# A two-layer Mamba/attention kernel on one core: where the two layer norms of layer 1 get their sums, and new due times

## The chip, the cores and the metric

One Trainium2 chip, one of its cores. A core has TensorE (PE in the profile), VectorE (DVE), ScalarE (ACT), GpSimd (POOL) and a queue engine, SyncE (SP), that here issues almost all DMAs. Each engine works through its own instructions in program order and waits on semaphores for the others. The metric is the device time of one execution in microseconds (us), less is better; all data is fp32.

## The reference

The input `x` has 8 images of 384 channels and 32 x 32 = 1024 positions. Layer 0 is an RMS norm, a Mamba block run forwards and backwards over the 1024 positions (16 states a channel), and a gated depthwise 3 x 3 convolution, all added to `x`. Layer 1 works on tokens and is

```python
t = _to_tokens(x)
t = t + _L1_attn_ref(_ln_t(t), L1_attn_Wq, L1_attn_Wk, L1_attn_Wv)
t = t + _L1_ffn_ref(_ln_t(t), L1_ffn_c_fc_1, L1_ffn_c_fc_2, L1_ffn_c_proj_1, L1_ffn_c_proj_2)

def _ln_t(v, eps=1e-5):
    m = jnp.mean(v, axis=-1, keepdims=True)
    s = jnp.var(v, axis=-1, keepdims=True)
    return (v - m) / jnp.sqrt(s + eps)
```

The attention is causal with 64-wide rotated queries and keys; the feed-forward has 1536 hidden units, an exact GELU, and weights that are Kronecker products. The change touches only how `m` and `s` of `_ln_t` are made (two norms, each over 384 channels of 8 x 1024 tokens, so 128 tiles of 128 tokens in all) and when things are scheduled.

## The kernel before, in words

**Staging.** The eight images are a software pipeline. For image `b` the scan of layer 0 runs in four steps (`STEPS`: two halves of 512 positions, backwards and forwards), each of 12 units (`NU * SG`, three channel tiles times four state groups), so 48 units an image and 384 in all. One unit (`scan`) is: a GpSimd product `hs = du * br` over 128 x 2048; four ScalarE exponentials `da = exp(dl * nega)` into PSUM; four VectorE scans (`tensor_tensor_scan`); the product with `cr`, on VectorE in four pieces or, for the units in `POOL_C`, on GpSimd in one piece; and four TensorE matmuls with `sel` that add the states up into the PSUM bank `y`. While one image scans, the next image's norm, projections and convolutions (`arrive`, `conv_tokens`, `prepare`, `local_branch`) and the previous image's layer 1 (`attention`, `feed_forward`) are laid between its units. After the last image's scan only its own layer 1 is left.

**What sets the order.** No engine's order is written out. Every call goes through `plan.scalar`, `plan.vector` and so on, and is recorded with a due time in scan units (`plan.due`) and a priority bonus (`plan.rush`). `Plan.order()` then schedules all recorded operations with its own costs, one list per engine, and `issue()` emits them in that order; that is why nearly every row of the profile has line L494, the one call in `issue()`. An operation's rank is its due less its rush: among those that could start, the lowest rank goes first. The constants at the head of the file are such due times: `FIRST`, `SECOND`, `OTHERS` for the next image's preparation, `PROJECT` for the last projection of layer 0, `LAYER1` and `LAYER1_7` for attention and feed-forward, `EXPS` the rush of the exponentials, `SCAN` the offsets within a unit, `DU_AHEAD` and `DL_AHEAD` how far ahead the scan's inputs are loaded. `PATIENCE` and `YIELD` weigh a switch of ScalarE's function table. There are five PSUM banks for `da` (`DAS`), two for everything else (`w`) and one for `y`. Where TensorE would idle long enough to lose clock, the planner puts in matmuls by zero (`y<-zero,ident`).

**The lines around the change.** `project` (L1171) writes one tile of the layer-1 input, `t1[:, ti]` (128 tokens x 384 channels), by a ScalarE copy out of PSUM. `token_norm` (from L1175) makes the statistics of `nt` tiles (4, or 2 in the last half): per tile a VectorE `bn_stats` and `bn_aggr`, which give mean and variance; then on ScalarE `Ln` and `Exp` (the power -1/2), an operation `minus`, and one 128 x 1 operation per tile for the bias. `normed` applies both in one ScalarE pass into `xt` (two buffers), which TensorE transposes. `attention` adds its result to `t1` by a VectorE `scalar_tensor_tensor` (L1318), and `feed_forward` calls `token_norm` again on that. The profile calls `t1` by `t`.

Of the kernel before, what the change touches and what calls it, by code (L numbers as in the profile page):

```python
# [26 lines left out]
AF = mybir.ActivationFunctionType  # L27
ALU = mybir.AluOpType
AX = mybir.AxisListType

P = 128
# [10 lines left out]
LATER_US = 36.0  # L42


FIRST = (2.72, 6.32, 10.68, 12.81, 18.74, 20.85)
SECOND = (22.85, 0.56)
OTHERS = (
    (3.96, 9.04, 14.9, 17.84, 20.11, 24.16, 30.75, 28, 43.27, 52.42),
    (3.99, 9.04, 15.17, 17.84, 20.3, 24.1, 30.14, 30.73, 43.27, 52.45),
    (3.99, 8.8, 14.02, 17.77, 20.08, 25.25, 30.19, 27.95, 42.89, 51),  # L50
    (3.99, 9.04, 14.9, 17.84, 19.59, 24.12, 30.52, 30.81, 42.97, 52.39),
    (3.99, 8.7, 15.25, 17.84, 20.1, 24.57, 29.82, 28, 43.27, 52.42),
    (3.99, 8.21, 14.9, 17.77, 20.1, 24.12, 30.52, 26.96, 43.27, 51.49),
    (3.82, 8.84, 15.11, 17.55, 20.38, 24.12, 29.69, 27.74, 41.51, 52.45),
)
BURST = 8.31
PROJECT = (2.31, 2.01, 2.15, 1.76, 2.22, 1.78, 2.15, 2.22, 0.91)
LAYER1 = (
    (38.52, 47.93, 60.93, 69.79, 84.06),
    (38.04, 48.09, 60.67, 69.2, 83.95),  # L60
    (38.63, 48.04, 61.04, 69.31, 84.17),
    (38.33, 47.57, 60.93, 69.59, 84.06),
    (41.08, 45.96, 60.93, 69.71, 84.06),
    (38.16, 48.76, 60.73, 69.67, 83.84),
    (44.98, 47.51, 53.66, 70.69, 74.67),
)
LAYER1_7 = (39.27, 42.31, 50.52, 59.01, 62.44, 70.84, 71.42, 76.4, 81.79)
HASTE = 25.1
FREE = ["w", "da", "w", "da"]
EXPS = -0.37  # L70
SCAN = (-1.43, -1.16, -0.47, -0.43, -0.26, 0.17, 0.01, 1.1, 0.64)
DU_AHEAD = 2.82
DL_AHEAD = 2.15
DLS = 5
DAS = 5
class _Op:
# [21 lines left out]
class Plan:  # L98
# [8 lines left out]
    SWITCH = 1.4  # L107
    LOOSE = ("w", "tmp", "wt")
    HURRY = 7.14
    PATIENCE = 1.81  # L110
    TAIL = dict(tensor=0.21, vector=0.117, scalar=0.14, gpsimd=0.1, sync=0.1)
    RAW = 0.07
    NEXT = 0.01
    SIGHT = 48.0
    YIELD = 6.02
    TURN = 0.1
    RATE = 320e3
    LEAD, FIX, LAND = 1.2, 0.1, 2.0
# [379 lines left out]
def conv_attn_kernel(  # L498
# [20 lines left out]
    nc = tc.nc  # L519
    NB, C, H, W = x.shape  # L520
    L = H * W
# [13 lines left out]
    NT = HB // P  # L535
# [4 lines left out]
    l1 = ctx.enter_context(tc.tile_pool(name="l1", bufs=1))  # L540
# [18 lines left out]
    plan = Plan(nc, tc)  # L559
# [5 lines left out]
    eps = const.tile([P, 2], F32, name="eps")  # L565
# [99 lines left out]
    pa = bank()[:, : C // CG * NS]  # L665
# [481 lines left out]
    def project(b, h, t1, lo=0, hi=HB):  # L1147

        yz = [yz_t[b, h, lo, cc] for cc in range(NC)]
        wout = heavy("wout", b)  # L1150
        lx = []
        for cc in range(NC):
            lx.append((tmp()[:, : hi - lo], reps()[:, : hi - lo]))
            plan.sync.dma_start(lx[cc][0], lx_t[b, h][cc * P : (cc + 1) * P, lo:hi])
            plan.sync.dma_start(lx[cc][1], xv[b, :, cc, h * HB + lo : h * HB + hi])
        yield
        for i in range((hi - lo) // P):
            cols = slice(i * P, (i + 1) * P)
            po = bank()
            for cc in range(NC):  # L1160
                plan.tensor.matmul(
                    po[:, :C], yz[cc][:, cols], wout[:, cc], start=cc == 0, stop=False,
                    skip_group_check=True,
                )
            for cc in range(NC):
                for k in range(2):
                    plan.tensor.matmul(
                        po[:, cc * P : (cc + 1) * P], lx[cc][k][:, cols], ident, start=False,
                        stop=cc == NC - 1 and k == 1, is_transpose=True, skip_group_check=True,
                    )  # L1170
            plan.scalar.copy(t1[:, h * NT + lo // P + i], po[:, :C])  # L1171
            yield


    def token_norm(t1, ti0, nt):  # L1175

        mv = plan.tile(l1, [P, NT, 2], "mv")[:, :nt]
        for i in range(nt):
            st = plan.tile(l1, [P, nc.vector.BN_STATS_DIM], "st", 2)
            plan.vector.bn_stats(st, t1[:, ti0 + i])  # L1180
            plan.vector.bn_aggr(mv[:, i], st)
        nrm = plan.tile(l1, [P, 2, NT], "nrm", 2)[:, :, :nt]
        plan.scalar.activation(nrm[:, 0], mv[:, :, 1], AF.Ln, bias=eps[:, 1:2])
        plan.scalar.activation(nrm[:, 0], nrm[:, 0], AF.Exp, scale=-0.5)
        minus = plan.tile(l1, [P, NT], "minus", 2)[:, :nt]
        plan.scalar.activation(minus, nrm[:, 0], AF.Identity, scale=-1.0)
        for i in range(nt):
            plan.scalar.activation(
                nrm[:, 1, i : i + 1], mv[:, i, 0:1], AF.Identity, scale=minus[:, i : i + 1]
            )  # L1190
        return nrm

# [5 lines left out]
        )  # L1198
        return xt

    kv_t = {}

    def attention(b, t1, t0, n, end=False):
        if b not in kv_t:
# [4 lines left out]
        k_all, v_all = kv_t[b]  # L1209
        half = slice(t0, t0 + n)  # L1210
        tile0, nt = t0 // P, n // P
        nrm = token_norm(t1, tile0, nt)
        yield
        if end:
            xT = plan.tile(l0, [P, NQ * HB], "hs", 5)[:, : NC * n]
# [3 lines left out]
        for i in range(nt):  # L1219
            xt = normed(t1, tile0, nrm, i)  # L1220
# [45 lines left out]
        for i in range(nt):  # L1266
            ti = tile0 + i
            spans = [(s, min(s + HB, (ti + 1) * P)) for s in range(0, (ti + 1) * P, HB)]
            ng = len(spans)
            sm = plan.tile(l1, [P, 8], "sm", 2)  # L1270
            scores = []
            for g, (s0, s1) in enumerate(spans):
                pg = bank()
                diag = g == ng - 1
                plan.tensor.matmul(
                    pg[:, : s1 - s0], q[:, i * P : (i + 1) * P], k_all[:, s0:s1],
                    start=True, stop=not diag,
                )
                if diag:
                    plan.tensor.matmul(  # L1280
                        pg[:, s1 - s0 - P : s1 - s0], ident, cmask, start=False, stop=True
                    )
                plan.vector.reduce_max(sm[:, g : g + 1], pg[:, : s1 - s0], axis=AX.X)
                scores.append(pg)
            if ng == 2:
                plan.vector.reduce_max(sm[:, 3:4], sm[:, 0:2], axis=AX.X)
            top = sm[:, 3:4] if ng == 2 else sm[:, 0:1]
            plan.vector.tensor_scalar_mul(sm[:, 2:3], top, -sscale)
            pr = []
            for g, (s0, s1) in enumerate(spans):  # L1290
                pr.append(plan.tile(l1, [P, HB], "p", 2))
                plan.scalar.activation(
                    pr[g][:, : s1 - s0], scores[g][:, : s1 - s0], AF.Exp,
                    bias=sm[:, 2:3], scale=sscale, accum_out=sm[:, 4 + g : 5 + g],
                )
            yield
            total = sm[:, 4:5]
            if ng == 2:
                total = sm[:, 7:8]
                plan.vector.reduce_sum(total, sm[:, 4:6], axis=AX.X)  # L1300
            plan.vector.reciprocal(sm[:, 6:7], total)
            pT = []
            for g, (s0, s1) in enumerate(spans):
                pg = bank()
                for s in range(s0, s1, P):
                    plan.tensor.transpose(
                        pg[:, s - s0 : s - s0 + P], pr[g][:, s - s0 : s - s0 + P], ident
                    )
                pT.append(plan.tile(l1, [P, HB], "p", 2))
                plan.scalar.copy(pT[g][:, : s1 - s0], pg[:, : s1 - s0])  # L1310
            yield
            pa = bank()
            for j in range(ti + 1):
                plan.tensor.matmul(
                    pa[:, :C], pT[j // NT][:, j % NT * P : (j % NT + 1) * P], v_all[:, j],
                    start=j == 0, stop=j == ti,
                )
            plan.vector.scalar_tensor_tensor(  # L1318
                t1[:, ti], pa[:, :C], sm[:, 6:7], t1[:, ti], ALU.mult, ALU.add
            )  # L1320
            yield

    def feed_forward(b, t1, t0, n, direct=False):
        tile0, nt = t0 // P, n // P
        nrm = token_norm(t1, tile0, nt)
        yield

        xT = plan.tile(l1, [P, NF // 2, HB], "gl")[:, :NC, :n]
        for i in range(nt):
            xt = normed(t1, tile0, nrm, i)  # L1330
# [95 lines left out]
    for b in range(NB):  # L1426
# [32 lines left out]
            local_branch(b, 1, v[8], v[9])  # L1459

        t1 = plan.tile(l1, [P, L // P, C], "t1")
        for si, (d, h) in enumerate(STEPS):

            parts = ((0, HQ), (HQ, HB)) if last and si == 3 else ((0, HB),)
            for lo, hi in parts:
                e = B + (si + hi / HB) * NU * SG
                scan(b, si, lo, hi)
                if si >= 2:
                    rota[:] = FREE if last and si == 3 and hi == HB else ["w"]
                    plan.rush = HASTE if last else 0.0  # L1470
                    plan.spread(project(b, h, t1, lo, hi), e + 0.45, e + PROJECT[b + (lo > 0)])
                    plan.rush = 0.0
# [90 lines left out]
```

## Time and profile before

| | |
|---|---|
| runs | 2993.01, 2996.16, 2999.89 us; median 2996.16 |
| the profiled execution | 2996.29 us, of it span 2994.5 us from first to last instruction; mean granted TensorE clock 0.963 |
| DMA | 674.54 MB, queue of SyncE busy 67.6% of 16 engines' span |
| the four scan instructions on VectorE, busy | 631.0 + 595.0 + 325.8 + 307.0 us |
| `hs<-hs,br` on GpSimd | 399 instructions, 1739.7 us |
| `da<-dl,nega` (the exponentials) on ScalarE | 1584 instructions, 1040.5 us |
| table loads on ScalarE | 163, 1283 ns each |
| matmuls by zero on TensorE | 1620 records, 428.1 us |

A row of a group reads: line, engine, operation, output <- inputs by name, shapes, how many; then busy us and mean ns of one; then the engine's idle time just before them and what ended it. Instructions of one engine overlap a little at their ends, so busy times of groups, added up, can exceed the engine's.

### The profile page before, as it was taken

How to read it: one execution, taken by the hardware profiler on the slowest of the kernel's cores; microseconds unless marked ns; L12 is line 12 of the kernel's file. 1: busy time of each engine (PE TensorE's matmuls, PEld its weight loads, DVE VectorE, ACT ScalarE, POOL GpSimd, SP SyncE). 2: the span in 40 equal slices, each digit the busy share in tenths (PEclk: the TensorE clock that was granted, in tenths of full speed). 3: DMA queues.
4: the chain of work that ended last, by engine and by line, in shares of the span. 5: the costliest groups of instructions: out<-in, count | busy, mean ns of one | idle time of the engine just before them, and what ended most of it. 6: DMA issues, size and time to landing. Idle time of an engine off the chain costs nothing. (4 is left out here: it accounts for less than half of the span.)

```text
span 2994.5 us, 40605 instructions
## 1 busy us (share of the span) xinstructions
PE 2748.8 (92%) x12560; PEld 1245.8 (42%) x12560; DVE 2662.6 (89%) x3443; ACT 2225.2 (74%) x4166; POOL 2505.5 (84%) x692
## 2 busy tenths in 40 slices
PE   8779789999999889999999998999999998998899
PEld 4334244443444334343444434343343434444455
DVE  5799779898999899998999989999899989999971
ACT  4666567778697887878787786877778786777674
POOL 3899788698888888899988888889789889999840
PEclk9989899999999999999999999999899999999999
DMA  6778886668767687687867686676776778543510
GB/s 205 274 266 259 299 277 226 210 239 272 231 226 250 237 268 230 224 271 233 267 201 245 215 294 208 214 259 232 261 235 216 263 248 256 181 153 124 175 55 11
DMA packets 371490, 674.54 MB, mean 225 GB/s; under 512 B 44640, under 2 KB 73640, under 8 KB 371272
## 3 DMA queue, kind: packets, MB, share of 16 engines
q1 hardware_dynamic: 371144, 671.83, 67.6%
q8 instruction: 99, 1.62, 0.2%
q14 instruction: 119, 0.97, 0.1%
q0 software_dynamic: 128, 0.11, 0.0%
HBM read 505.60 MB, written 166.18 MB: 224 GB/s over the span
## 5 line engine op out<-in xcount | busy, mean ns | idle before, releaser
L494 POOL TENSOR_TENSOR hs<-hs,br 128x2048 f32<-128x2048 f32 (+2 forms) x399 | 1739.7, 4378 | 245.7 <-PE y L494 136.3
L494 ACT ACTIVATE da<-dl,nega 128x512 f32<-128x512 f32 (+1 forms) x1584 | 1040.5, 678 | 270.6 <-DVE hs L494 237.2
L494 POOL TENSOR_TENSOR hs<-hs,cr 128x2048 f32<-128x2048 f32 (+1 forms) x137 | 599.6, 4377 | 130.3 <-DVE hs L494 75.9
L494 DVE TENSOR_TENSOR_SCAN da<-da,carry,hs 128x512 f32<-128x512 f32 (+1 forms) x532 | 631.0, 1221 | 66.3 <-POOL hs L494 48.7
L494 DVE TENSOR_TENSOR hs<-da,cr 128x512 f32<-128x512 f32 (+1 forms) x1036 | 658.5, 666 | 2.1
L494 DVE TENSOR_TENSOR_SCAN da<-da,hs 128x512 f32<-128x512 f32 x504 | 595.0, 1217 | 38.9 <-ACT da L494 28.2
L494 PE MATMUL y<-hs,sel 128*32 128x512 f32 (+1 forms) x3168 | 427.3, 606 | 41.8 <-POOL hs L494 37.5
L494 PE MATMUL y<-zero,ident 128*128 128x256 f32 x1620 | 428.1, 394 | 0.0
L494 PEld LDWEIGHTS y<-zero,ident 128*128 128x128 f32 x1620 | 291.0, 193 | 160.1 <-issue 128.8
L494 DVE TENSOR_TENSOR_SCAN hs<-da,hs 128x512 f32<-128x512 f32 x264 | 307.0, 1208 | 51.0 <-ACT da L494 49.7
L494 DVE TENSOR_TENSOR_SCAN hs<-da,carry,hs 128x512 f32<-128x512 f32 (+1 forms) x284 | 325.8, 1191 | 12.6 <-ACT da L494 11.7
L494 PE MATMUL w<-xn,wt 128*128 128x512 f32 x576 | 268.0, 607 | 3.4 <-ACT tmp L494 1.7
L492 ACT ACT_TABLE_LOAD x162 | 207.8, 1283 | 2.9
L494 PE MATMUL w<-v,p 128*128 128x384 f32 x562 | 198.4, 499 | 3.9 <-ACT p L494 2.5
L494 PEld LDWEIGHTS y<-hs,sel 128*32 128x32 f32 x3168 | 90.4, 111 | 259.1 <-issue 136.4
L494 ACT COPY carry<-da 128x1 f32<-128x1 f32 x532 | 77.5, 161 | 152.6 <-DVE hs L494 151.4
L494 PE MATMUL w<-q,fc1s 32*128 32x512 f32 (+1 forms) x396 | 161.2, 679 | 28.2 <-ACT gl L494 13.4
L494 ACT COPY gl<-w 128x384 f32<-128x384 f32 (+2 forms) x317 | 160.3, 537 | 30.5 <-PE w L494 30.0
L494 PEld LDWEIGHTS w<-xn,wt 128*128 128x128 f32 x576 | 105.9, 193 | 142.9 <-issue 107.3
L494 PE MATMUL w<-rep,cit 96*32 96x512 f32 x1152 | 151.4, 639 | 4.6 <-ACT gl L494 2.8
L494 PE MATMUL y<-tmp,ddiag 128*128 128x512 f32 (+1 forms) x198 | 115.6, 669 | 43.5 <-DVE tmp L494 19.4
L494 PEld LDWEIGHTS w<-v,p 128*128 128x128 f32 x562 | 103.5, 192 | 90.3 <-ACT p L494 19.5
(187 smaller groups left out, 3349.2 us busy)
## 6 DMA issues: line engine op xcount, KB each, us to landing
hs<-db SPq DMA_DIRECT2D x372, 256.0 KB, 4.7
dl<-dd SPq DMA_DIRECT2D x372, 256.0 KB, 4.2
rep<-up SPq DMA_DIRECT2D x180, 257.5 KB, 4.2
rep<-xq SPq DMA_DIRECT2D x192, 222.4 KB, 4.8
br<-bd SPq DMA_DIRECT2D x124, 256.0 KB, 4.5
cr<-bd SPq DMA_DIRECT2D x124, 256.0 KB, 4.8
ud<-uc SPq DMA_DIRECT2D x96, 256.0 KB, 4.4
dd<-tmp SPq DMA_DIRECT2D x96, 256.0 KB, 4.0
```

The lines of the kernel that those rows point to most:

```text
L492: self.nc.scalar.preload_act_table_set(table)
L494: op.call(*args, **{k: self._bind(v) for k, v in op.kw.items()})
```

## The change

The statistics of `_ln_t` are made by ScalarE. The ScalarE pass that writes `t1` in `project` becomes an `Identity` activation with an accumulator output, the row sum; the VectorE instruction that adds attention's result to `t1` gets an accumulator output too. `token_norm` takes the sums, has VectorE multiply them by -1/C (one small instruction for all tiles of the norm: `mean` holds minus the mean), and lets ScalarE square each tile about its mean with an accumulator output, the sum of squares `var`; `1/C` goes into the scale of the `Ln`. `bn_stats`, `bn_aggr` and `minus` go. The pass of squares writes into the `xt` buffers and uses nothing of what it writes. The due times are others.

```diff
-FIRST = (2.72, 6.32, 10.68, 12.81, 18.74, 20.85)
+FIRST = (3.34, 6.32, 11.21, 12.81, 18.69, 20.85)
...
-    (3.96, 9.04, 14.9, 17.84, 20.11, 24.16, 30.75, 28, 43.27, 52.42),
+    (4.1, 9.04, 14.9, 17.84, 20.11, 24.88, 29.66, 30.73, 43.27, 52.42),
...
-BURST = 8.31
-PROJECT = (2.31, 2.01, 2.15, 1.76, 2.22, 1.78, 2.15, 2.22, 0.91)
+BURST = 7.93
+PROJECT = (2.31, 2.01, 2.22, 0.98, 1.75, 1.6, 2.15, 2.22, 0.91)
...
-LAYER1_7 = (39.27, 42.31, 50.52, 59.01, 62.44, 70.84, 71.42, 76.4, 81.79)
+LAYER1_7 = (40.42, 42.2, 51.27, 58.72, 62.92, 71.14, 71.84, 76.4, 80.71)
...
-EXPS = -0.37
-SCAN = (-1.43, -1.16, -0.47, -0.43, -0.26, 0.17, 0.01, 1.1, 0.64)
-DU_AHEAD = 2.82
-DL_AHEAD = 2.15
+EXPS = -1.3
+SCAN = (-1.43, -1.18, -0.47, -0.43, -0.26, 0.17, 0.01, 1.1, 0.66)
+DU_AHEAD = 2.93
+DL_AHEAD = 2.71
...
-    PATIENCE = 1.81
+    PATIENCE = 1.76
...
-    YIELD = 6.02
+    YIELD = 5.89
...
-            plan.scalar.copy(t1[:, h * NT + lo // P + i], po[:, :C])
+            ti = h * NT + lo // P + i
+            plan.scalar.activation(
+                t1[:, ti], po[:, :C], AF.Identity, accum_out=sums_t[b][:, ti : ti + 1]
+            )
...
-    def token_norm(t1, ti0, nt):
-
-        mv = plan.tile(l1, [P, NT, 2], "mv")[:, :nt]
+    def token_norm(b, t1, ti0, nt):
+
+        mean = plan.tile(l1, [P, NT], "mean", 2)[:, :nt]
+        plan.vector.tensor_scalar_mul(mean, sums_t[b][:, ti0 : ti0 + nt], -1.0 / C)
+        var = plan.tile(l1, [P, NT], "var", 2)[:, :nt]
         for i in range(nt):
-            st = plan.tile(l1, [P, nc.vector.BN_STATS_DIM], "st", 2)
-            plan.vector.bn_stats(st, t1[:, ti0 + i])
-            plan.vector.bn_aggr(mv[:, i], st)
+            sq = plan.tile(l1, [P, C], "xt", 2)
+            plan.scalar.activation(
+                sq, t1[:, ti0 + i], AF.Square, bias=mean[:, i : i + 1],
+                accum_out=var[:, i : i + 1],
+            )
         nrm = plan.tile(l1, [P, 2, NT], "nrm", 2)[:, :, :nt]
-        plan.scalar.activation(nrm[:, 0], mv[:, :, 1], AF.Ln, bias=eps[:, 1:2])
+        plan.scalar.activation(nrm[:, 0], var, AF.Ln, bias=eps[:, 1:2], scale=1.0 / C)
         plan.scalar.activation(nrm[:, 0], nrm[:, 0], AF.Exp, scale=-0.5)
-        minus = plan.tile(l1, [P, NT], "minus", 2)[:, :nt]
-        plan.scalar.activation(minus, nrm[:, 0], AF.Identity, scale=-1.0)
         for i in range(nt):
             plan.scalar.activation(
-                nrm[:, 1, i : i + 1], mv[:, i, 0:1], AF.Identity, scale=minus[:, i : i + 1]
+                nrm[:, 1, i : i + 1], mean[:, i : i + 1], AF.Identity, scale=nrm[:, 0, i : i + 1]
             )
         return nrm
...
             plan.vector.scalar_tensor_tensor(
-                t1[:, ti], pa[:, :C], sm[:, 6:7], t1[:, ti], ALU.mult, ALU.add
+                t1[:, ti], pa[:, :C], sm[:, 6:7], t1[:, ti], ALU.mult, ALU.add,
+                accum_out=sums_t[b][:, ti : ti + 1],
             )
...
         t1 = plan.tile(l1, [P, L // P, C], "t1")
+        sums_t[b] = plan.tile(l1, [P, L // P], "sums", 2)
```

Left out of the diff: the other six rows of `OTHERS` (the sixth entry moves from about 24.1 to about 24.9, the eighth from 27 to 30.8 to 29.8 to 30.8, the rest by some tenths), small moves in `LAYER1`, and the parameter `b` at the two calls of `token_norm`. In the built programs VectorE goes from 3445 listed instructions to 3223 (128 `bn_stats` and 128 `bn_aggr` less, 34 `mean` more), ScalarE from 4072 to 4168 (128 squares more, 34 `minus` less, table loads 163 to 165), TensorE has 825 instead of 810 matmuls by zero, GpSimd and SyncE have as many as before; accumulator reads are not among the listed ones. The order changes on every engine.

## The prediction

> **What bounds the kernel now.** I read the busy sums first, then busy times by stretch, then VectorE's waits, then the groups that the change touches. The sums of the page:
>
> ```profile
> span 2994.5 us, 40605 instructions
> ...
> PE 2748.8 (92%) x12560; PEld 1245.8 (42%) x12560; DVE 2662.6 (89%) x3443; ACT 2225.2 (74%) x4166; POOL 2505.5 (84%) x692
> ```
>
> TensorE looks fullest, but 428.1 us of its time are matmuls by zero that the planner put into gaps; without them it is at 78%. VectorE is the fullest engine with work that counts. The busy times by stretch (us from the span's start, stretch length, then busy us per engine, granted clock, DMA share, GB/s):
>
> ```profile
> 0.00:100.00 100.00, 85.59 (x266) 38.79 (x266) 63.45 (x118) 48.89 (x86) 48.51 (x28) 0.97 0.69 227
> 100.00:450.00 350.00, 284.68 (x1239) 116.30 (x1240) 285.33 (x321) 227.04 (x377) 299.41 (x87) 0.90 0.81 274
> 450.00:2880.00 2430.00, 2271.18 (x10501) 1028.26 (x10499) 2282.37 (x2931) 1885.69 (x3566) 2152.73 (x577) 0.97 0.69 228
> 2880.00:2995.00 115.00, 107.36 (x558) 62.43 (x556) 31.49 (x76) 63.59 (x140) 4.89 (x3) 0.99 0.07 22
> ```
>
> The columns are PE, PEld, DVE, ACT, POOL. In the long middle VectorE is busy 94%, GpSimd 89%, ScalarE 78%. It idles 147.6 us there; the same view in 50 us stretches shows 30 of 49 with VectorE at 47 us or more, several at the full 50. In the last 115 us it is nearly idle: the last image's layer 1 is bound by TensorE and ScalarE in turn. What VectorE waited for in the middle (us, times, longest):
>
> ```profile
> DVE hs L494 <- ACT da L494: 44.1, 22, 6.3
> DVE da L494 <- ACT da L494: 34.5, 18, 5.7
> DVE da L494 <- POOL hs L494: 24.5, 11, 9.2
> DVE tmp L494 <- PE y L494: 23.2, 11, 8.1
> ```
>
> So VectorE sets the pace of the middle, and what stops it most (78.6 us in 40 waits) is a late exponential from ScalarE, the engine that now gets more to do. The same view for GpSimd gives 104.7 us on `y` (a `hs` buffer freed by TensorE), 58.3 on VectorE and 46.2 on ScalarE's `carry`: it waits for the loop that VectorE paces.
>
> **What is taken off VectorE.** The groups:
>
> ```profile
> L494 DVE BATCH_NORM_STATS2 st<-t 128x6 f32<-128x384 f32 x128 | 68.3, 548 | 5.8 <-ACT t L494 5.7
> ...
> L494 DVE BATCH_NORM_AGGREGATE mv<-st 128x2 f32<-128x6 f32 x128 | 21.2, 172 | 1.3 <-ACT nrm L494 1.0
> ...
> L494 DVE RECIPROCAL sm<-sm 128x1 f32<-128x1 f32 x64 | 9.8, 153 | 0.2
> ...
> L494 DVE TENSOR_SCALAR sm<-sm 128x1 f32<-128x1 f32 x64 | 9.2, 144 | 0.1
> ```
>
> and what a place in the queue really costs, from VectorE's timeline (start, us):
>
> ```profile
> 1159.14 0.54 DVE L494 BATCH_NORM_STATS2 st<-t 128x6 f32<-128x384 f32 x1
> 1159.59 0.67 DVE L494 TENSOR_TENSOR hs<-da,cr 128x512 f32<-128x512 f32 x1
> 1160.18 0.17 DVE L494 BATCH_NORM_AGGREGATE mv<-st 128x2 f32<-128x6 f32 x1
> 1160.27 0.53 DVE L494 BATCH_NORM_STATS2 st<-t 128x6 f32<-128x384 f32 x1
> ```
>
> Each starts 0.09 before the one ahead has ended. 117 of the 128 tiles lie in the middle (62.4 + 19.3 us by the same groups there), so 81.7 - 234 x 0.09 = 60.6 us of VectorE's queue go.
>
> **What is put on VectorE.** About 30 `mean` products in the middle; the nearest row is the `TENSOR_SCALAR` at 144 ns, less 90 in the queue: 30 x 0.054 = 1.6 us. 60 adds `t<-w,sm,t` get an accumulator output. No row shows one on this engine. Below: nothing (another output can't shorten the pass). Above: a read of its own as long as ScalarE's, 194 ns, so 60 x 0.194 = 11.6 us. I take the nearest small VectorE row, `RECIPROCAL`, 153 less 90: 60 x 0.063 = 3.8 us. The Trainium skill (VectorE: DVE Perf Modes, Two Vector instructions with no wait between them) says that an operation which writes out its accumulator is two instructions, the second a read; no VectorE row of this trace shows it. By it alone the term is nearer 3.8 than 0.
>
> Net 60.6 - 1.6 - 3.8 = 55.2 us off VectorE's queue in the middle.
>
> **What of that shows.** Of the 79.6 us that the statistics show as busy in those 49 stretches, 54.8 lie in the 30 where VectorE is at 47 of 50 or more, 69%. There I let it count in full: 0.69 x 55.2 = 38 us. The other 17 lie where another engine stops VectorE anyway: between 0 and 17, I take half. Together -46 us (bounds -38 and -55).
>
> **What is put on ScalarE.**
>
> ```profile
> L494 ACT ACTIVATE xt<-t,nrm 128x384 f32<-128x384 f32 x128 | 87.6, 705 | 0.0
> ...
> L494 ACT ACTIVATION_READ_ACCUMULATOR p<-w,sm 128x1 f32 x94 | 18.2, 194 | 0.0
> ```
>
> The square is not in the trace. `xt<-t,nrm`, the same tile with two pointer operands, takes 705 ns: above. Copies of 512 and 384 columns from PSUM differ by 585 - 479 = 106 ns, so `da<-dl,nega` (690 ns at 512 in the timeline, one pointer, from SBUF like the square) would be 584 at 384 columns: I take that, and 479 (no pointer, from PSUM) as the lower bound. Ends overlap by some 0.1 us, the accumulator read too (0.194, of which 0.10 stays in the timeline): 117 x (0.49 + 0.10) = 69 us. The accumulator reads of 57 passes that write `t`: 57 x 0.10 = 6. Two more table loads: 2.6. The 30 `minus` go: -30 x 0.23 = -7. About +70 us, ScalarE from 1885.7 to 1956 of some 2390: its idle share falls from 22% to 18%.
>
> What waits behind a square are the exponentials, and behind those VectorE's scans. If the added time is no worse than the average ScalarE microsecond, it brings 78.6/1885.7 = 4% of it as VectorE idle: 70 x 0.04 = 3 us. If waits grow as idle shrinks, 78.6 x (22.4/18.2 - 1) = 18 us. Bounds 0 (the squares fall into idle time, 544 us of it) and 70. I take 10. `EXPS` from -0.37 to -1.3 lets other work of ScalarE go ahead of exponentials by 0.93 units more, against it; `DL_AHEAD` from 2.15 to 2.71 brings their inputs sooner, for it. The rest of the dues I cost at nothing, with +-15 us in the range: first loads and projections move by under one unit (some 7.6 us), the local branch from about 28 to 30.7 units, and no transfer or operation is added or taken by them.
>
> The skill (ScalarE: Activation LUTs, Rules for kernel authors) speaks against the whole move: multiplications and additions belong on VectorE. Going by it, 70 us bought with 55 would be a loss of 15, which holds if both engines were full; here one idles 6% and the other 22%, and the stretch rows decide.
>
> **The tail.** In the last 115 us the norm is on the chain. Now: `t` written at 2956.18, `Ln` at 2957.26, 1.08 us later. After: accumulator read 0.15, `mean` 0.15, two squares one behind the other 2 x 0.59 and the last read 0.1, two changes of engine of some 0.1 each: 1.8, less `minus` 0.23. +0.5 us for each of the four norms there, +2 us; bounds 0 and 6.
>
> **Sum.** The profiled execution took 2996.29 us (1.8 outside its span; 0.13 above the median, so no correction): 2996 - 46 + 10 + 2 = **2962 us**.
>
> **Rivals.**
> *More than the queue time comes back (21%).* VectorE's waits for GpSimd's `hs` (24.5) and for `y` (23.2) are knots of the due times, and moving the local branch and the loads undoes half of them, -24; with all 55 shown, +10 and +2: 2953 at the least change and 2929 with the knots. For it: 9.2 and 8.1 us are single waits, so a few places. Against: nothing says that the new order has fewer.
> *GpSimd paces instead (10%).* The scan's loop is held by `hs` buffers that pass from GpSimd over VectorE to TensorE; then VectorE's time turns into waits for `hs`. Only a fifth shows: -11 + 2 = 2987; with the ScalarE term of 10 on top 2997, no change. For it: GpSimd is at 89%, and 95 us of 100 in some stretches. Against: 277 us idle there, most of it waiting for TensorE and VectorE's loop.
> *ScalarE's lateness takes the place (17%), slower.* Squares come four at a time with their reads, some 2.4 us a norm, plus a gelu with two table loads (1.28 + 2.77 + 1.28 = 5.3) in the same layer, while five `da` banks hold some 8 us of VectorE work (5 scans of 1.2, most of their 5 products of 0.6). If the whole 70 lies ahead of exponentials that VectorE needs: 2996 - 46 + 70 + 2 = 3022. It decides against the change from 46 - 2 = 44 us of added waits, that is when `ACT da` waits pass 123 us instead of 78.6. Against: ScalarE itself idles 198.3 us in 208 waits for VectorE to free `da` banks.
>
> **How the numbers follow.** The forecast has 52%, 2940 to 2985. To hold 8 of 10 the range takes in most of the two neighbours and the start of the slow case: 2922 to 3004. A measurement of this kernel can't tell less than 0.2%, 6 us, from no change. Faster by more: 52 + 21 + 5 (half of GpSimd's) = 78%. Within: the other 5. Slower: 17.
>
> **What would show it.** Right: in the middle VectorE's share stays at 93 to 95% with about 55 us less of it, `ACT da` waits at 80 to 100 us; `READ_ACCUMULATOR` rows on ScalarE rise from 96 to 288; the square at about 585 ns. Wrong if VectorE's idle in the middle grows beyond 190 us, if `POOL hs` leads its waits, or if the first 450 us, where no norm runs before 380, change by over 10 us: then the due times did it.

## The result: slower by 2.4%

| | median us (runs) | ratio to before, 95% interval |
|---|---|---|
| before | 2998.02 (2993.01 to 3003.45) | |
| after | 3071.87 (3061.77 to 3079.77) | 1.0244 [1.0201, 1.0288] |

The forecast was 2962, the range 2922 to 3004. The change lost 74 us where 34 were to be won. The busy sums of the page after (the profiled execution took 3061.77 us, the fastest of the four):

```profile
span 3060.0 us, 40878 instructions
...
PE 2782.7 (91%) x12590; PEld 1257.1 (41%) x12590; DVE 2645.5 (86%) x3285; ACT 2294.8 (75%) x4454; POOL 2505.8 (82%) x692
```

VectorE lost all of `bn_stats` and `bn_aggr`, 89.5 us by their rows, and yet its sum fell by only 17 (2662.6 to 2645.5). Something new takes up the rest. What VectorE and then ScalarE waited for (us, times, longest):

```profile
DVE hs L494 <- ACT da L494: 92.0, 40, 7.2
DVE da L494 <- ACT da L494: 85.1, 34, 6.7
DVE da L494 <- POOL hs L494: 47.6, 16, 12.9
```

```profile
ACT xt L494 <- DVE mean L494: 33.5, 12, 4.6
```

Waits of VectorE for exponentials went from 103 us (61.4 + 41.7 in the whole span before) to 177, and ScalarE's squares wait 33.5 us for `mean`, a product over four columns. The rows of the new instructions on VectorE and ScalarE:

```profile
L494 DVE TENSOR_SCALAR mean<-sums 128x4 f32<-128x4 f32 x30 | 53.2, 1776 | 0.6 <-ACT t L494 0.6
...
L494 DVE DVE_READ_ACCUMULATOR t<-w,sm,t 128x1 f32 x63 | 5.2, 82 | 0.0
```

```profile
L494 ACT ACTIVATE xt<-t,mean 128x384 f32<-128x384 f32 x128 | 77.5, 607 | 33.6 <-DVE mean L494 33.5
...
L494 ACT ACTIVATION_READ_ACCUMULATOR xt<-t,mean 128x1 f32 x128 | 24.4, 190 | 0.0
```

The square (607 ns, forecast 585) and ScalarE's accumulator read (190, forecast 194) are as forecast, and VectorE's read (82 ns) lies between the bounds given for it. The mean product is not: 1776 ns for four elements per partition, where the row of a 128 x 1 product had 144. The view of the tile `mean` shows how uneven it is:

```profile
L494 DVE TENSOR_SCALAR mean<-sums x34: 141/546/5035, 392.6 to 3021.0; 128x4 f32<-128x4 f32 x30, 128x2 f32<-128x2 f32 x4
```

That is the shortest, median and longest in ns. One of the long ones on VectorE's timeline, and GpSimd's over the same time (start, us):

```profile
2452.24 0.69 DVE L494 TENSOR_TENSOR hs<-da,cr 128x512 f32<-128x512 f32 x1
2452.85 3.29 DVE L494 TENSOR_SCALAR mean<-sums 128x4 f32<-128x4 f32 x1
2456.05 0.74 DVE L494 SCALAR_TENSOR_TENSOR tmp<-y,gs,tmp 128x512 f32<-128x512 f32 x1
```

```profile
2442.56 18.15 POOL L494 TENSOR_TENSOR hs<-hs,br 128x2048 f32<-128x2048 f32 x4
```

GpSimd ran four products of 4.54 us without a break; the third ended at 2442.56 + 3 x 4.54 = 2456.2, and `mean` at 2456.14. Of the 34 mean products 17 took over 0.7 us, 53.2 of the 55.9 us together, and each of the 17 ended within 0.1 us of the end of a GpSimd instruction; one more, of 0.32 us, did too. All 18 had begun inside a GpSimd instruction. The 16 short ones (141 to 170 ns) ran while GpSimd was idle or at a change between its instructions. So the product waits for GpSimd. That is the first theory: a lock between the two engines. The Trainium skill (SBUF — State Buffer, Who interferes with whom) says so: VectorE in a mode that uses both its SBUF ports shares one pair with GpSimd, the pair is held for a whole instruction, `tensor_scalar` is among the operations that can enter the mode, and the other side blocks. The trace agrees for 17 of the 18, which end with the very GpSimd instruction that they began beside; the longest, 5.04 us, waited through two more (last section).

### The profile page after: what moved, and what is told of

It is laid out like the page before. It is cut to its first block, busy times and chain, and to the rows that moved or that the text cites. A ratio compares the mean times of both kernels' runs of the same rounds, so it can differ in the third digit from the quotient of the medians.

```text
span 3060.0 us, 40878 instructions
## 1 busy us (share of the span) xinstructions
PE 2782.7 (91%) x12590; PEld 1257.1 (41%) x12590; DVE 2645.5 (86%) x3285; ACT 2294.8 (75%) x4454; POOL 2505.8 (82%) x692
## 5 line engine op out<-in xcount | busy, mean ns | idle before, releaser
L494 POOL TENSOR_TENSOR hs<-hs,br 128x2048 f32<-128x2048 f32 (+2 forms) x399 | 1739.9, 4377 | 295.8 <-PE y L494 161.4
L494 POOL TENSOR_TENSOR hs<-hs,cr 128x2048 f32<-128x2048 f32 (+1 forms) x137 | 599.6, 4376 | 133.2 <-ACT carry L494 65.9
L494 PE MATMUL y<-hs,sel 128*32 128x512 f32 (+1 forms) x3168 | 443.5, 605 | 44.2 <-POOL hs L494 34.2
L494 PE MATMUL w<-wt,tmp 128*128 128x384 f32 x378 | 136.7, 498 | 12.6 <-DVE tmp L494 7.4
```

Source lines behind the costliest of these rows:

```text
L494: op.call(*args, **{k: self._bind(v) for k, v in op.kw.items()})
```

## The experiments

Where nothing else is said, every engine's order is that of the kernel it starts from: the edit changes only what a recorded operation emits.

### The mean product, and the due times

**One column at a time**, in the changed kernel (here and below, `...` stands for lines left out of an edit):

```diff
-        plan.vector.tensor_scalar_mul(mean, sums_t[b][:, ti0 : ti0 + nt], -1.0 / C)
+        plan.add("vector", columns, "tensor_scalar_mul", (mean, sums_t[b][:, ti0 : ti0 + nt], -1.0 / C), {})
...
+    def columns(out, in_, by):
+        for i in range(out.shape[1]):
+            nc.vector.tensor_scalar_mul(out[:, i : i + 1], in_[:, i : i + 1], by)
```

> The changed kernel, every engine's order kept, but each mean product of 128 x 4 (or x 2) is issued as four (two) products of 128 x 1. Lock theory: the 128 x 4 product waits for the GpSimd instruction in flight (in the changed kernel's trace each long one ends within 0.1 us of the end of a GpSimd instruction), 34 x (1.65 - 0.15) = 51 us of VectorE, and ScalarE's squares wait for it 33.5 us; one column at a time does not wait: mean rows at some 145 ns, median time 2960 to 3005. Rival, the due times made a worse order: falls by less than 15 us, 3055 or more. Rival, ScalarE's added 100 us of passes set the pace: the same, 3055 or more, with VectorE's waits for the exponentials still near 177 us.

Measured: 3002.11 us, ratio to before 1.0012 [1.0001, 1.0022]. The row:

```profile
L1180 DVE TENSOR_SCALAR mean<-sums 128x1 f32<-128x1 f32 x128 | 10.6, 143 | 4.5 <-ACT t L494 4.5
```

Nearly four times the instructions, a fifth of the time: 80 of the 128 run wholly inside a GpSimd instruction, and none takes over 155 ns. 70 us come off, with the same order and due times, and ScalarE's wait for `mean` goes from 33.5 us to 0.5. The lock is nearly all of the loss. But what is left is no gain.

**The wide product added to the kernel before**, behind the last `bn_aggr` of each norm, used by nobody:

```diff
+    def closing(out, in_):
+        nc.vector.bn_aggr(out, in_)
+        nc.vector.tensor_scalar_mul(spare, ones[:, :NT], -1.0 / C)
...
-            plan.vector.bn_aggr(mv[:, i], st)
+            plan.add("vector", closing if i == nt - 1 else nc.vector.bn_aggr, "bn_aggr", (mv[:, i], st), {})
```

> The kernel before, order kept, with one 128 x 4 product of a constant on VectorE behind the last bn_aggr of each norm (34 in all; nobody uses it). Lock theory: a mean of 1 to 2 us each, 34 to 68 us of VectorE where it is the fullest engine: 3030 to 3075. Rivals (due times, ScalarE's load): 34 x 0.06, nothing measurable, 2990 to 3005.

> Control: the same as the run with the wide product, but as four 128 x 1 products (136 in all). Lock theory: no waits, 136 x 0.06 = 8 us at most, 2995 to 3010. If any small product behind bn_aggr costs (its place in the queue, not its width), it is as slow as the wide one.

Measured: wide 3060.8, ratio 1.0207 [1.0188, 1.0226]; as columns 3001.76, ratio 1.0013 [1.0002, 1.0025]. The two rows:

```profile
L1178 DVE TENSOR_SCALAR spare<-ones 128x4 f32<-128x4 f32 x34 | 72.0, 2116 | 0.0
```

```profile
L1179 DVE TENSOR_SCALAR spare<-ones 128x1 f32<-128x1 f32 x136 | 10.3, 137 | 0.0
```

34 instructions of four elements, on which nothing depends, cost 62 us; the same four elements of each partition in four pieces cost 3. Width, not place or count, makes the wait. Here too every product that began inside a GpSimd instruction with more than 0.2 us to run waited (22 of them).

**The due times alone**: the kernel before with every constant of the changed one (and so another order).

> The kernel before with bn_stats and bn_aggr, but all due times, PATIENCE and YIELD of the changed kernel. Lock theory: the due times carry little, 2980 to 3020. Rival, the due times are what slowed it: 3040 or more.

Measured: 3052.33, ratio 1.0167 [1.0142, 1.0192]. My expectation of the lock theory fell: the due times carry a lot. The other half, the changed kernel with columns and the old due times:

> The changed kernel with mean in columns of 128 x 1, and all due times, PATIENCE and YIELD of the kernel before. Theory 'due times fit only the statistics they stand with' (as the kernel before lost 54 us with the new ones): 3020 to 3060. Rival, the new due times are worse in themselves: 2950 to 2985, below both kernels.

Measured: 3061.13, ratio 1.0219 [1.0203, 1.0236], just above the range expected. So neither set is worse in itself. Each fits its own statistics better: old with old 2998, new with new (without the lock) 3002, either mixture 3052 to 3061.

**Another plan**: the kernel before with three small moves (`BURST`, `PATIENCE` and `YIELD` as in the changed kernel), and so a new order.

> The kernel before with three small moves only: BURST 8.31 to 7.93, PATIENCE 1.81 to 1.76, YIELD 6.02 to 5.89. Control for what any other plan costs. If any replanning costs: 3015 or more. If the 54 us of the new due times come from their content: 2985 to 3010.

Measured: 3022.28, ratio 1.0083 [1.0062, 1.0104]. This disturbance of the plan alone costs 24 us, nearly half of what the new due times cost. One such run doesn't tell how much of their 54 us comes from what they say and how much from any new order.

### What an engine's time is worth

**50 us off one engine**, in the order of the kernel before. VectorE:

```diff
-            plan.vector.bn_stats(st, t1[:, ti0 + i])
+            plan.add("vector", short, "bn_stats", (st, t1[:, ti0 + i]), {})
...
+    def short(out, in_):
+        nc.vector.bn_stats(out, in_[:, :8])
```

> The kernel before, order kept, with bn_stats over 8 of the 384 channels (wrong statistics; 376 of 384 channels left out of them): 128 x 0.39 = 50 us off VectorE and nothing added elsewhere. The prediction's step that VectorE paces the middle: 0.83 of it shows, 2998 - 35 to 45, 2950 to 2965. Rival, the other engines give it back in this order: 2985 or more.

Measured: 2981.35, ratio 0.9961 [0.9939, 0.9984], between the two ranges named. GpSimd and TensorE in the same manner (`hs * cr` over 469 of 512 positions, `y` over 448 of 512):

> The kernel before, order kept, with GpSimd's 137 products with cr over 469 of every 512 positions (it leaves that factor out of 43 of 512): 137 x 0.37 = 50 us off GpSimd, as the short bn_stats took some 50 off VectorE and gave 14. Theory 'GpSimd and not VectorE paces the scan': 2996 falls by 30 us or more. Rival 'no single engine does; each waits for the others in its fixed order': 5 to 25 us.

> The kernel before, order kept, with TensorE's state sums (y from sel and hs) over 448 of 512 positions (it leaves the sum out for 64 of 512): some 53 us of 427 off TensorE. Theory 'TensorE paces, full as it looks': 30 us or more come off. Rival 'no single engine does': 0 to 25 us.

Measured: GpSimd 2989.86, ratio 0.9981 [0.9968, 0.9993]; TensorE 2991.66, ratio 0.9983 [0.9971, 0.9994]. By the busy sums 44 us were taken from VectorE (2662.6 to 2618.3), 47 from GpSimd and 20 from TensorE (53 were meant), and 14, 8 and 6 us came off the time, against the runs of the kernel before beside each. None of the three paces the kernel alone: VectorE and TensorE give about a third of what they lost, GpSimd a sixth. The page of the run with short `bn_stats`, and VectorE's waits there:

```profile
PE 2737.9 (92%) x12560; PEld 1242.1 (42%) x12560; DVE 2618.3 (88%) x3443; ACT 2225.7 (75%) x4166; POOL 2505.5 (84%) x692
```

```profile
DVE hs L494 <- ACT da L494: 68.5, 31, 6.3
DVE da L494 <- POOL hs L494: 53.4, 18, 12.7
DVE da L494 <- ACT da L494: 46.3, 22, 6.7
```

VectorE is done sooner and idles 28 us longer (span less busy time, 360.0 for 331.9), 12 of them in waits for exponentials (114.8 for 103.1). Most of the freed time is given back in later waits.

**ScalarE's share of the squares**, in the order of the changed kernel with columns: each square over 8 of 384 channels.

> The run with mean in columns, every engine's order kept, but each pass of squares covers 8 of the 384 channels (the variance is then wrong; it leaves 376 of 384 squares out): 128 x 0.31 = 40 us less on ScalarE. Theory 'ScalarE's lateness gave VectorE's gain back': 3002 falls by 20 to 45 us, 2957 to 2982, and VectorE's waits for exponentials go from 172 to about 130 us. Rival, the squares lie in ScalarE's idle time and the waits come from the order alone: 2993 to 3005.

Measured: 2999.39, ratio 1.0015 [1.0005, 1.0025] (with full squares 1.0012). ScalarE's sum fell by 34 us (2294.0 to 2259.8) and nothing came of it: in the new order the width of the squares lies where ScalarE has time. The instructions themselves, 0.29 us each when short, were still there.

**The new statistics in the old order.** The kernel before, its due times and order kept; what the old operations emit is changed: row sums with the writes of `t`, a 128 x 1 mean where `bn_aggr` stood, the squares in front of the `Ln`:

```diff
+        def emit(out, in_, func, bias):
+            for i in range(out.shape[1]):
+                nc.scalar.activation(
+                    junk, plan._bind(t1[:, ti0 + i]), AF.Square, bias=mean[:, i : i + 1],
+                    accum_out=var[:, i : i + 1],
+                )
+            nc.scalar.activation(out, var, func, bias=bias, scale=1.0 / C)
```

> The kernel before with every engine's order and due times kept, and the new statistics put into the old places: the copy that writes t and attention's add take the row sum along, each mean is a 128 x 1 product in the place of its bn_aggr, the four squares stand in front of the Ln, bn_stats and minus are gone. Theory 'the statistics alone are worth little: 14 us from VectorE, 3 us lost on ScalarE; the changed kernel without the lock is even only because its new order is worth some 15 us less': 2980 to 2993, below both kernels. Rival, ScalarE's added passes (100 us) cost what VectorE gains: 2995 or more.

> The same, but the mean of a norm is one ScalarE pass over 128 x 4 in front of its squares, so VectorE does none of the statistics but the sum taken along: 34 x 0.2 us more on ScalarE, 128 x 0.06 less on VectorE, and no change of engine between sum, mean and square. 2978 to 2993, within 4 us of the run with the mean on VectorE.

Measured: 3074.26, ratio 1.0252 [1.0228, 1.0275]; with the mean on ScalarE 3091.01, ratio 1.0302 [1.0279, 1.0325]. Both expectations fell, by 80 us and more. ScalarE's timeline in the first:

```profile
1200.95 0.60 ACT L1168 ACTIVATE junk<-t,mean 128x384 f32<-128x384 f32 x1
1201.46 0.19 ACT L1168 ACTIVATION_READ_ACCUMULATOR junk<-t,mean 128x1 f32 x1
1201.68 0.61 ACT L1168 ACTIVATE junk<-t,mean 128x384 f32<-128x384 f32 x1
...
1203.91 0.30 ACT L1172 ACTIVATE nrm<-var,eps 128x4 f32<-128x4 f32 x1
```

Four squares hold ScalarE for 3 us in one piece, 0.74 us each (0.22 from the start of the read to the next square, where the changed kernel has 0.1; all write one `junk` tile here, so each probably waits for the one ahead). To tell that time from the count of instructions and from the rest of the new statistics, squares over 8 channels, and none:

> The run with the new statistics in the old order (3074), with each square over 8 of 384 channels (376 of 384 left out of the variance): 128 x 0.31 = 40 us less on ScalarE, the same 128 + 128 instructions in the same four-in-a-row. Theory 'what costs is ScalarE's time in front of exponentials': falls in proportion to the block's length, from 3.0 to 1.8 us, by 25 to 45 us to 3030 to 3050. Rival 'the count of instructions or the changed chain t - mean - square costs, not their time': 3065 or more.

> The same without the 128 squares (one 128 x 4 pass stands in for them; the variance is left out): VectorE freed of bn_stats and bn_aggr, ScalarE with the 64 accumulator reads only. Theory: 2975 to 2995, VectorE's relief of some 14 us less what the reads cost. Rival: 3030 or more, something else in the new statistics is slow (the sum taken along, the mean's place).

Measured: 3027.54, ratio 1.0098 [1.0072, 1.0124], and 2990.58, ratio 0.9975 [0.9961, 0.9988]. The first fell by 47 us, a little more than the 25 to 45 expected; the count of instructions as the whole cost is out. The rest of the new statistics is a small gain, 7 us, for 54 us off VectorE (2662.6 to 2608.3). The squares cost 3074 - 2991 = 84 us for 128 x 0.74 = 95 us of ScalarE, and the short ones 37 us for 128 x 0.42 = 54 us: 0.7 to 0.9 us lost for each us put into ScalarE's queue at a place that the plan had given to others. Their width alone cost 47 us here, for 41 of ScalarE's busy sum (2313.8 to 2272.8); in the new order 34 us of the same width cost nothing. VectorE's waits in the run with full squares:

```profile
DVE hs L494 <- ACT da L494: 103.9, 47, 8.1
DVE da L494 <- ACT da L494: 86.5, 42, 6.6
```

190 us, for 103 before and 130 without squares (76.5 + 53.1). No version beat both kernels with its whole computation in it.

## Why the prediction was wrong, step by step

**The cost of `mean` failed, and that made the loss.** The step was "About 30 `mean` products in the middle; the nearest row is the `TENSOR_SCALAR` at 144 ns", 1.6 us. It measured 55.9 us in all and 70 us of the kernel's time. VectorE's own waiting is 51 us of it (55.9 less 34 x 0.14); in the kernel before, where nothing needs the product, 67 us of such waiting cost 62. ScalarE's 33.5 us of waits for `mean` come on top; VectorE's waits for exponentials hardly depend on it (177 us with the lock, 172 without). The row was the nearest by name but not by shape: 128 x 1, while `mean` is 128 x 4 or 128 x 2. The trace before had no `tensor_scalar` of more than one column while GpSimd ran (the last such `tensor_scalar` starts at 45.5 us, GpSimd's first `hs` at 51), so it could not show the price, and no upper bound was set. One GpSimd product of 4.4 us for each, 34 x 4.4 = 150 us, would have put a clear loss into the range. Without the lock the changed kernel is level with the one before, 3002 to 2999; why it is no gain is the next step's matter.

**"VectorE sets the pace of the middle" failed, and that took the gain.** I counted 46 of 55 us as shown. Measured: 14 of 44 in the fixed order, 7 of 54 with the rest of the new statistics. What was taken off was sized rightly: with the mean in columns VectorE is busy 2228.0 us from 450 to 2880, 54 less than before, and all 54 are idle time there. A share of 94% busy didn't mean that the engine paces; most of the 147.6 us of idle time there were waits for three other engines, and that idle time grew when VectorE had less to do. The same test on GpSimd and TensorE rules out each of them as the single pace too.

**ScalarE's 10 us was the right mechanism with a size that has no single value.** In the old order, four in a row, the squares cost 84 us, above my bound of 70; in the new order their width is worth 3 at most. The new order places them otherwise, and its squares write two buffers by turns; no run separates the two. The slower rival, "ScalarE's lateness takes the place", named the wait and its sign (over 123 us of waits for exponentials in the middle decide against; from 450 to 2939 us, the same stretch, it is 152), but the changed kernel is even without the lock, so these waits are not what made it slow. After columns they are still 172 us over the whole span (91.2 + 81.1) at 3002 us: 69 more than before, about the 63 us by which VectorE is less busy (2662.6 to 2600.0).

**"The rest of the dues I cost at nothing, with +-15 us" failed.** Taken alone they cost 54 us, and with the new statistics they save 59. The reading that they make room for the squares fits the 47 us that the squares' width costs in the old order and the nothing that it costs in the new one; no run shows it by itself. The forecast's sign for the due times, the first 450 us, could not see this: VectorE had done 192 of its 1584 scan instructions at 435 us before and at 441 after. Another of its signs did show: VectorE's idle time in the middle passed 190 us (213 from 450 to 2939).

**What held.** The counts, the square at 607 ns (forecast 585), the accumulator reads, and the tail, where one norm at a time stands on the path: from the end of the last write of `t` on VectorE to the start of its `Ln` it took 1.08 us before (2956.18 to 2957.26 on the timeline) and 2.01 after (3020.93 to 3022.94), 0.93 more for this norm. The forecast was 0.5, so some 4 us over four norms, if all are like it, in place of 2. The tail as a whole lost 7, most of it with the due times and not with the norms: from the end of the last scan instruction to the end of the span it took 96.8 us before, 103.6 after, 104.1 with the old statistics under the new due times, and 99.8 with the new ones in the old order.

**Put together.** New statistics without squares -7, squares at unplanned places +84, the new order -72 (3074 to 3002; the squares write two buffers by turns there), the lock +70: +75. Each step goes from one measured kernel to the next, so the sum comes to the measured +74 by itself and proves nothing about the names of the steps; the lock has its own proof above, the name of the -72 is a reading. What stays open is what the best order for the new statistics would give: the two orders at hand are single draws, and one small disturbance of the old one costs 24 us.

## What to carry to other kernels

Where GpSimd streams through SBUF, look at every `tensor_scalar` of VectorE from SBUF to SBUF that is wider than one column, however small (128 x 4 and 128 x 2 are the shapes seen here; no odd width above one was tried): price it at a whole GpSimd instruction until a run shows otherwise, and, where it has few columns, issue it as 128 x 1 pieces. In a program whose order was fixed ahead, time is priced by its place: here 44 us off the fullest engine gave 14, while time put where the plan had none cost 0.7 to 0.9 us per us on ScalarE and 0.9 on VectorE (62 us for 67 of waiting). Test an engine for being the pace by shortening its work in the same order before building a change on its busy share.

## What was not expected of the hardware

A 128 x 4 `tensor_scalar` in SBUF takes 141 to 5035 ns beside GpSimd's 4.4 us products (mean 1648), a 128 x 1 one 143 on average beside the same. The longest, 5.04 us, began while GpSimd ran products of 2.3 us back to back and passed over two ends of such instructions before it got its turn (VectorE's line, then GpSimd's):

```profile
2861.35 5.04 DVE L494 TENSOR_SCALAR mean<-sums 128x4 f32<-128x4 f32 x1
```

```profile
2859.37 2.37 POOL L494 TENSOR_TENSOR hs<-hs,cr 128x1024 f32<-128x1024 f32 x1
2861.68 4.67 POOL L494 TENSOR_TENSOR hs<-hs,br 128x1024 f32<-128x1024 f32 x2
```

In the kernel before with the wide product two waits were longer still, 11.0 and 10.7 us, past four and two such ends. So one GpSimd instruction is not an upper bound; why a waiting product misses an end stays open. GpSimd's own products show nothing of it: 4377 ns before, 4376 after.
